# One sum of eight heads' softmax denominators in place of two sums of four, and a later place for the last one, in a fused attention and convolution kernel

## The chip, the cores and the metric

The kernel runs on one core of a Trainium2 chip, as one program. The metric is the device time of one execution, in microseconds (us). The compute engines are TensorE (PE, matrix products), VectorE (DVE), ScalarE (ACT) and GpSimd (Pool). SyncE (SP) computes nothing; its queue starts DMA transfers, as Pool's and ACT's queues can too.

## The reference

Two layers follow each other on an input of 4 images with 1024 channels and 32 x 32 pixels. The first is self-attention over the 1024 pixels (tokens) of an image, with 16 heads of 64 channels. The second is a bottleneck of three convolutions with batch normalization. All is float32. The change concerns the first layer, and in it the softmax:

```python
qkv = (x @ w_qkv.T + b_qkv).reshape(B, N, 3, nh, hd)
q, k, v = (qkv[:, :, 0], qkv[:, :, 1], qkv[:, :, 2])
q = _apply_rope(q, cos, sin)
k = _apply_rope(k, cos, sin)
q = _rmsnorm(q.reshape(B, N, inner), q_norm_w).reshape(B, N, nh, hd)
k = _rmsnorm(k.reshape(B, N, inner), k_norm_w).reshape(B, N, nh, hd)
scores = jnp.einsum('bqhd,bkhd->bhqk', q, k) * scale
attn = jax.nn.softmax(scores, axis=-1)
ctx = jnp.einsum('bhqk,bkhd->bqhd', attn, v).reshape(B, N, inner)
out = ctx @ w_proj.T
out = _rmsnorm(out, norm_out_w)
out = out + residual
```

After it come a 1x1 convolution to 256 channels, a 3x3 convolution and a 1x1 convolution back to 1024 channels, each with batch normalization over the whole batch, and a residual.

## The kernel before

The four images (batches 0 to 3) are worked through one after the other. For each of them the kernel projects q, k and v, does the attention, and projects the result with w_proj (the output projection, matmuls that the profile calls `p_y`). The four dense products of the layer use a Strassen-like scheme with seven products in place of eight, hence the many sums and differences on DVE.

Attention (`attention`) goes through two halves of 512 queries each (`c` = 0, 1), and in each half through eight pairs of heads (`hp` = 0 to 7). For a pair it makes eight score tiles `sc` of 128 keys by 2 heads by 512 queries (L781, four matmuls that share the array), ACT takes the exponential of each into `p` (L788), and DVE adds the eight tiles into one array of denominators of 128 partitions by 2 heads by 512 queries, `den` (L799 and L801). Then PE multiplies the eight tiles by v into `cx` (L810). The softmax is not divided before that product. Instead the context that comes out is multiplied by the inverse of its denominator later, in `mean_of_v`: a multiplication on DVE (L764) and the addition of v's bias on Pool (L765).

Before it can be inverted, a denominator has to be summed over the 128 partitions. This is a matmul with a matrix of ones, `dn`, into a bank of the pool `sc`, which has three tiles that go round. There are two ways:

- `sums_of_four`: four matmuls for the four heads of two pairs (L863), each with 128 partitions. `inverses` follows it: an ACT copy (L910), a transfer to DRAM and back into a shape with more partitions (L898, L902), a short reciprocal on DVE (L914), and transfers that spread each row over 64 partitions (L915, L932). The last group of a batch is treated by `last_inverses`, with a long reciprocal on DVE (L924) and Pool's queue for the transfers (L925, L932).
- `sum_of_eight`: `halve` first adds the upper 64 partitions of each pair's denominators to the lower 64 by accumulating DMAs on Pool's queue. For an even pair this is one copy (L873), for an odd pair two (L875 and then L876, which adds onto what L875 wrote). The result lies in a "home", one of the tiles T0 and T2. Four matmuls then do eight heads (L882), and the ACT copy is at L884 and the short reciprocal at L889.

Batch 0 uses the first way everywhere. Batches 1 to 3 use `sum_of_eight` in the first half of queries (`fold[0]`, two homes) and `sums_of_four` in the second half (`fold[1]` is None).

The order of the work is written out by hand: on PE, Pool, DVE and ACT the instructions stand in the order in which the program emits them. What is put off goes through lists. `late` holds sums of four, made after the second score tile of the next pair. `eights` holds sums of eight and `half_done` holds inversions, each with the number of the pair (8c + hp) at whose end it is due. `ready` holds spread inverses, taken by `mean_of_v` at the end of the next odd pair. In the projections, `after(n, step)` runs a step when n products have been done, where one matmul group of the output projection counts as half a product. `then` and `means` there are the differences for the first products and the `mean_of_v` of the last heads, on DVE. At each odd pair's end the program emits first `mean_of_v`, then `halve`, then what is due from the lists. `slow` puts the previous batch's residual additions (L1254, DMAs on Pool's queue) at pair ends.

The projections use the pools `o1` and `o2` of four banks each, in the same eight banks of PSUM as attention's `sc` and `cx`; a bank waits for its last reader.

Of the kernel before, what the change touches and what calls it, by code (L numbers as in the profile page):

```python
# [11 lines left out]
F32 = mybir.dt.float32  # L12
# [6 lines left out]
P = 128  # L19
# [66 lines left out]
def program(ctx, tc, x, wblk, w2, w3, vecs, cos, sin, out, bad):  # L86
# [71 lines left out]
    with tc.tile_pool(name=f"st{u}", bufs=2) as st, ExitStack() as s:  # L158
# [44 lines left out]
        def bank(kind, name):  # L203
            pool, shape = psum[kind]
            return pool.tile(shape, F32, tag=kind, name=name)
# [561 lines left out]
        def attention(b, c, q_all, k_all, v, probs_, late, ready, extra, slow, steps_in_all, load_parts, fold, then):  # L767


            at = half[c]  # L770
            sums_, contexts = [], []
            for hp in range(NHP):
                n = f"{b}_{c}_{hp}"
                rows = shifts(q_all, k_all, n, hp, c) if bad is None else None
                probs = []
                for t in range(N // P):
                    p = probs_[:, t]
                    sc = bank("sc", f"sc_{n}_{t}")
                    for keys in (low, high):
                        for j, d in enumerate((low, high)):  # L780
                            nc.tensor.matmul(  # L781
                                sc[keys, j], k_all[d, hp, t * P + keys.start : t * P + keys.stop], q_all[d, hp, at],
                                start=True, stop=bad is not None,
                            )
                    if bad is None:
                        for j in range(2):
                            nc.tensor.matmul(sc[:, j], ones[0:1, :], rows[j], start=False, stop=True)
                    nc.scalar.activation(p, sc, AF.Exp)  # L788
                    if t == 1:
                        if late:  # L790
                            late.pop(0)()
                        if fold and hp % 2 == 0:
                            d_ = fold[hp // 4][:, hp % 4 // 2 * 2 : hp % 4 // 2 * 2 + 2, :]
                        else:
                            d_ = acc.tile([P, 2, CH], F32, tag="tot", name=f"den_{n}")
                    if t == 3:
                        load_parts()
                    if t == 1:
                        nc.vector.tensor_tensor(d_, probs[0], p, ALU.add)  # L799
                    elif t > 1:  # L800
                        nc.vector.tensor_tensor(d_, d_, p, ALU.add)  # L801
                    probs.append(p)
                if (c, hp) == (NCH - 1, NHP - 1):
                    then()
                o = bank("cx", f"cx_{n}")
                for t in range(N // P):
                    for j in range(2):
                        h0 = (2 * hp + j) * HD
                        for i, keys in enumerate((low, high)):
                            nc.tensor.matmul(  # L810
                                o[j * HD : (j + 1) * HD, i], v[keys, t, h0 : h0 + HD], probs[t][keys, j],
                                start=(t == 0), stop=(t == N // P - 1),
                            )

                cx = q_all[:, hp, at]
                nc.scalar.copy(cx, o[:, 0])  # L816
                if b == 0 and (c, hp) != (NCH - 1, NHP - 1):
                    other = temp(f"cx_{n}")
                    nc.scalar.copy(other, o[:, 1])
                    nc.gpsimd.dma_start(cx, other, accum_op=ALU.add)  # L820
                else:
                    contexts.append((cx, o[:, 1]))
                sums_.append(d_)
                if hp % 2 == 1:
                    for r in ready:
                        mean_of_v(q_all, *r)
                    ready.clear()
                if fold:
                    halve(hp, d_, fold[hp // 4][:, hp % 4 // 2 * 2 : hp % 4 // 2 * 2 + 2, :])
                    if hp % 4 == 3:  # L830
                        eights.append((hp + 2, lambda n=n, hp=hp: sum_of_eight(b, n, hp, fold[hp // 4], ready)))
                if half_done and half_done[0][0] <= c * NHP + hp:
                    half_done.pop(0)[1]()
                if slow:
                    slow.pop(0)()

                if waiting:
                    next_waiting()
                slots = NCH * NHP - 1
                if extra and steps_in_all == 0 and hp > 0:  # L840
                    extra.pop(0)()
                for _ in range(len(extra) - -(-steps_in_all * max(slots - 1 - c * NHP - hp, 0) // slots) if steps_in_all else 0):
                    extra.pop(0)()
                if contexts:
                    nc.vector.tensor_tensor(contexts[0][0], *contexts.pop(0), ALU.add)
                if eights and eights[0][0] <= c * NHP + hp:
                    eights.pop(0)[1]()
                if hp % 2 == 0 or fold:
                    continue
                if (c, hp) == (NCH - 1, NHP - 1):  # L850
                    last_inverses(b, c, hp, n, sums_of_four(n, sums_), ready)
                else:
                    late.append(lambda n=n, hp=hp, ds=sums_: inverses(b, c, hp, n, sums_of_four(n, ds), ready))
                sums_ = []

        def sums_of_four(n, sums_):
            if n == f"0_{NCH - 1}_{NHP - 1}":
                bank("sc", f"skip_{n}")
            dn = bank("sc", f"dn_{n}")[:, 0]
            for i, d_ in enumerate(sums_):  # L860
                for j in range(2):
                    q = slice((2 * i + j) * QH, (2 * i + j + 1) * QH)
                    nc.tensor.matmul(dn[q, :], ones[:, :QH], d_[:, j], start=True, stop=True)  # L863
            return dn
# [10 lines left out]
                nc.gpsimd.dma_start(home[high], d_[high])  # L875
                nc.gpsimd.dma_start(home[high], d_[low], accum_op=ALU.add)  # L876

        def sum_of_eight(b, n, hp, home, ready):

            dn = bank("sc", f"dn_{n}")[:, 0]  # L880
            for i in range(4):
                nc.tensor.matmul(dn[i * QH : (i + 1) * QH, :], halves, home[:, i, :], start=True, stop=True)  # L882
            r = temp(f"rec_{n}")
            nc.scalar.copy(r, dn)  # L884
            k = 2 * b * NCH * NHP + 2 * (hp - 3)
            few, rows = to_few(n, k, 8, r[:: QH // 2, :])

            def invert():
                nc.vector.reciprocal(few, few)  # L889
                nc.sync.dma_start(rows, few)  # L890
                for i in range(2):
                    at = k + 4 * i
                    spread(0, hp - 2 + 2 * i, n + f"_{i}", ready, [dens[at : at + 2, :], dens[at + 2 : at + 4, :]])

            half_done.append((hp + 3, invert))

        def to_few(n, k, rows_, r):
            nc.sync.dma_start(dens[k : k + rows_, :], r)  # L898
# [6 lines left out]
        def inverses(b, c, hp, n, dn, ready):  # L905


            r = temp(f"rec_{n}")
            k = 2 * ((b * NCH + c) * NHP + hp - 1)
            nc.scalar.copy(r, dn)  # L910
            few, rows = to_few(n, k, 4, r[::QH, :])

            def invert():
                nc.vector.reciprocal(few, few)  # L914
                nc.sync.dma_start(rows, few)  # L915
                spread(c, hp, n, ready, [dens[k + j : k + j + 3 : 2, :] for j in range(2)])

            half_done.append((0, invert))

        def last_inverses(b, c, hp, n, dn, ready):  # L920
            k = 2 * ((b * NCH + c) * NHP + hp - 1)
            r = temp(f"rec_{n}")
            nc.scalar.copy(r, dn)
            nc.vector.reciprocal(r, r)  # L924
            nc.gpsimd.dma_start(dens[k : k + 4, :], r[::QH, :])  # L925
            spread(c, hp, n, ready, [dens[k + j : k + j + 3 : 2, :] for j in range(2)], nc.gpsimd)

        def spread(c, hp, n, ready, rows, queue=nc.sync):

            w = big_temp(f"inv_{n}")  # L930
            for j in range(2):
                queue.dma_start(  # L932
                    w[j * HD : (j + 1) * HD, :].rearrange("p (i t) -> p i t", i=2), rows[j].partition_broadcast(HD)
                )
            for i in range(2):
                ready.append((c, hp - 1 + i, w[:, half[i]]))
# [261 lines left out]
        for b in range(B):  # L1198
# [62 lines left out]
            fold = [None, None]  # L1261
            if b > 0:

                fold[0] = [tp.tile([P, NH, CH], F32, tag=t, name=f"den_{b}_{t}") for t in ("T0", "T2")]
            tc_, two = [], []

            def then(b=b, q_all=q_all, tc_=tc_, two=two):
# [428 lines left out]
```

## Time and profile before

| what | value |
|---|---|
| three runs | 2648.97, 2652.34, 2653.42 us; median 2652.34 |
| the profiled execution | 2650.94 us, of which its span 2649.1 us |
| PE busy | 2626.4 us (99% of the span) |
| DVE, ACT, Pool busy | 2143.2, 1120.7, 472.1 us |
| score tiles on PE (L781) | 456.4 us, products with v (L810) 338.2 + 112.7 us |
| `dn` on PE, four heads (L863) | 160 records, 23.2 us |
| bias of v on Pool (L765) | 56 records, 110.1 us, 1985 ns each |
| long reciprocal on DVE (L924) | 4 records, 3346 ns each |
| copies of `halve` (L873, L875, L876) | 12 each, 2.8 to 6.2 us from issue to landing |

The profile lists, for one execution, every instruction of every engine with its start, length, source line and tiles, the wait before it and what ended that wait. "Busy" is the time in which an engine worked on at least one instruction. A float32 matmul leaves two records, so a group of four `dn` matmuls has eight. Ends of matmuls are modelled. The granted clock of PE is given as a share of full speed; its mean over the execution was 0.998.

### The profile page before, as it was taken

How to read it: one execution, taken by the hardware profiler on the slowest of the kernel's cores; microseconds unless marked ns; L12 is line 12 of the kernel's file. 1: busy time of each engine (PE TensorE's matmuls, PEld its weight loads, DVE VectorE, ACT ScalarE, POOL GpSimd, SP SyncE). 2: the span in 40 equal slices, each digit the busy share in tenths (PEclk: the TensorE clock that was granted, in tenths of full speed). 3: DMA queues.
4: the chain of work that ended last, by engine and by line, in shares of the span. 5: the costliest groups of instructions: out<-in, count | busy, mean ns of one | idle time of the engine just before them, and what ended most of it. 6: DMA issues, size and time to landing. Idle time of an engine off the chain costs nothing. (4 is left out here: it accounts for less than half of the span.)

```text
span 2649.1 us, 40551 instructions
## 1 busy us (share of the span) xinstructions
PE 2626.4 (99%) x15446; PEld 1627.8 (61%) x15446; DVE 2143.2 (81%) x2595; ACT 1120.7 (42%) x1568; POOL 472.1 (18%) x592
## 2 busy tenths in 40 slices
PE   9999999999999999999999999999999999999997
PEld 4448533488888333688886333888884335846843
DVE  5567899998887877888879767987988779877987
ACT  2222566423442565333343565233525564312266
POOL 2542244301011221100111222000111221020000
PEclk9999999999999999999999999999999999999999
DMA  8887787777667451457775541765774443683175
GB/s 286 289 255 204 218 257 239 245 221 238 185 181 212 87 102 41 143 173 225 190 200 143 93 86 26 223 206 174 193 214 86 82 104 90 208 279 92 64 240 205
DMA packets 252939, 463.66 MB, mean 175 GB/s; under 512 B 32193, under 2 KB 125169, under 8 KB 252737
## 3 DMA queue, kind: packets, MB, share of 16 engines
q1 hardware_dynamic: 196816, 287.80, 34.7%
q0 software_dynamic: 47856, 156.40, 23.7%
q10 hardware_dynamic: 8064, 16.78, 1.8%
q8 instruction: 125, 2.05, 0.3%
q14 instruction: 78, 0.63, 0.1%
HBM read 329.53 MB, written 97.01 MB: 161 GB/s over the span
## 5 line engine op out<-in xcount | busy, mean ns | idle before, releaser
L788 ACT ACTIVATE p<-sc 128x1024 f32<-128x1024 f32 x512 | 478.2, 1047 | 17.7 <-PE sc L781 17.5
L781 PE MATMUL sc<-q,k 64*64 64x512 f32 x4096 | 456.4, 591 | 0.0
L801 DVE TENSOR_TENSOR den<-den,p 128x1024 f32<-128x1024 f32 x312 | 385.5, 1236 | 37.6 <-ACT p L788 5.1
L810 PE MATMUL cx<-p,to 64*64 64x512 f32 x3072 | 338.2, 589 | 0.0
L781 PEld LDWEIGHTS sc<-q,k 64*64 64x64 f32 x4096 | 149.3, 132 | 294.2 <-ACT p L788 150.6
L810 PEld LDWEIGHTS cx<-p,to 64*64 64x64 f32 x3072 | 117.5, 133 | 212.1 <-issue 210.8
L480 PE MATMUL p_v<-w_v,x 128*128 128x256 f32 x928 | 210.2, 379 | 1.4 <-DVE x L451 0.7
L485 PE MATMUL p_y<-q,w_y 128*128 128x256 f32 x928 | 209.8, 379 | 0.7 <-issue 0.7
L485 PEld LDWEIGHTS p_y<-q,w_y 128*128 128x128 f32 x928 | 176.0, 190 | 27.9 <-issue 4.1
L480 PEld LDWEIGHTS p_v<-w_v,x 128*128 128x128 f32 x928 | 176.1, 190 | 26.8 <-DVE x L451 1.7
L816 ACT COPY q<-cx 128x512 f32<-128x512 f32 x64 | 37.5, 586 | 348.0 <-PE cx L810 348.0
L765 POOL TENSOR_SCALAR q<-q,vec 128x512 f32<-128x512 f32 x56 | 110.1, 1985 | 290.2 <-DVE q L764 290.2
L485 PE MATMUL p_q<-to,w_q 128*128 128x256 f32 x672 | 152.2, 379 | 0.0
L485 PE MATMUL p_k<-to,w_k 128*128 128x256 f32 x672 | 152.2, 379 | 0.0
L485 PEld LDWEIGHTS p_q<-to,w_q 128*128 128x128 f32 x672 | 127.4, 190 | 18.4 <-issue 1.2
L485 PEld LDWEIGHTS p_k<-to,w_k 128*128 128x128 f32 x672 | 127.4, 190 | 18.4 <-issue 1.2
L810 PE MATMUL cx<-p,rq 64*64 64x512 f32 x1024 | 112.7, 589 | 0.0
L1600 PE MATMUL c<-h,w 128*128 128x512 f32 x256 | 110.3, 592 | 0.5 <-ACT h L1503 0.5
L799 DVE TENSOR_TENSOR den<-p 128x1024 f32<-128x1024 f32 x52 | 63.5, 1222 | 42.6 <-ACT p L788 42.6
L801 DVE TENSOR_TENSOR den_T<-den_T,p 128x1024 f32<-128x1024 f32 x72 | 88.2, 1225 | 7.5
L485 PE MATMUL p_y<-to,w_y 128*128 128x256 f32 x384 | 90.1, 379 | 0.6 <-PE p_y L485 0.6
L727 POOL DMA_DIRECT2D k<-ks x64 | 57.9, 1093 | 181.6 <-ACT p L788 70.9
(499 smaller groups left out, 4340.0 us busy)
## 6 DMA issues: line engine op xcount, KB each, us to landing
w_v<-wd2f SPq DMA_DIRECT2D x112, 256.0 KB, 3.2
w_y<-wd2f SPq DMA_DIRECT2D x112, 256.0 KB, 3.3
w_q<-wd2f SPq DMA_DIRECT2D x84, 256.0 KB, 3.0
w_k<-wd2f SPq DMA_DIRECT2D x84, 256.0 KB, 2.9
wd2f<-w_pre POOLq DMA_DIRECT2D x68, 256.0 KB, 4.5
q<-qs POOLq DMA_DIRECT2D x64, 256.0 KB, 5.5
k<-ks POOLq DMA_DIRECT2D x64, 256.0 KB, 4.7
x1df<-y POOLq DMA_DIRECT2D x32, 512.0 KB, 5.2
```

The costliest lines, as they stand in the source:

```text
L480: nc.tensor.matmul(o[:, q].rearrange("p (g f) -> p g f", g=2), r[:, i, q * P : (q + 1) * P], wt[:, :, i, :], skip_group_check=True, **at,)
L485: nc.tensor.matmul(o[:, q], wt[:, q, i, :], r[:, i, :], skip_group_check=True, **at)
L727: nc.gpsimd.dma_start(dst[i::2, f, :], other[1 - i :: 2, :], accum_op=ALU.add)
L765: engine.tensor_scalar(cx, cx, col("bv", hp), None, ALU.add)
L781: nc.tensor.matmul(sc[keys, j], k_all[d, hp, t * P + keys.start : t * P + keys.stop], q_all[d, hp, at], start=True, stop=bad is not None,)
L788: nc.scalar.activation(p, sc, AF.Exp)
L799: nc.vector.tensor_tensor(d_, probs[0], p, ALU.add)
L801: nc.vector.tensor_tensor(d_, d_, p, ALU.add)
L810: nc.tensor.matmul(o[j * HD : (j + 1) * HD, i], v[keys, t, h0 : h0 + HD], probs[t][keys, j], start=(t == 0), stop=(t == N // P - 1),)
L816: nc.scalar.copy(cx, o[:, 0])
L1600: nc.tensor.matmul(os[i], w3t[k][f // NH][:, f % NH, :], h2[b, k][:, half[c]], start=(k == 0), stop=(k == NPT - 1),)
```

## The change

In batches 1 and 2 the second half of queries gets one home too (`fold[1] = homes[:1]`, tile T0), for its first four pairs. Their eight heads take `sum_of_eight`. Pairs 4 to 7 have no home and stay with `sums_of_four`.

Sums of eight and inversions now carry due numbers that depend on the half, and two new places look at the lists inside a pair: after the third score tile for `half_done`, after the sixth for `eights`. With the numbers of the second half (+0.5 and +1.5) the sum of pairs 0 to 3 stands after the sixth score tile of pair 4, and its inversion after the third of pair 5. The inversions of sums of four carry the number of the next pair where they had 0.

The last group (pairs 6 and 7) of batches 1 and 2 is emitted by `after(0.5, ...)`, which is after the first matmul group of the output projection, and takes a bank of `o2`. In batches 0 and 3 it stays where it was. An unused bank that batch 0 allocated before its last sum is gone.

```diff
             sums_, contexts = [], []
+            homes = fold
             for hp in range(NHP):
+                fold = homes if homes and hp // 4 < len(homes) else None
...
                     nc.scalar.activation(p, sc, AF.Exp)
+                    if t == 2 and half_done and half_done[0][0] < c * NHP + hp:
+                        half_done.pop(0)[1]()
+                    if t == 5 and eights and eights[0][0] < c * NHP + hp:
+                        eights.pop(0)[1]()
...
-                sums_.append(d_)
+                if not fold:
+                    sums_.append(d_)
...
                     halve(hp, d_, fold[hp // 4][:, hp % 4 // 2 * 2 : hp % 4 // 2 * 2 + 2, :])
                     if hp % 4 == 3:
-                        eights.append((hp + 2, lambda n=n, hp=hp: sum_of_eight(b, n, hp, fold[hp // 4], ready)))
+                        home = fold[hp // 4]
+                        eights.append(
+                            (c * NHP + hp + (2, 0.5)[c], lambda n=n, hp=hp, home=home: sum_of_eight(b, c, n, hp, home, ready))
+                        )
...
                 if (c, hp) == (NCH - 1, NHP - 1):
-                    last_inverses(b, c, hp, n, sums_of_four(n, sums_), ready)
+
+                    def last(ds=sums_):
+                        last_inverses(b, c, hp, n, sums_of_four(n, ds), ready)
+
+                    if 0 < b < B - 1:
+                        after(0.5, last)
+                    else:
+                        last()
...
         def sums_of_four(n, sums_):
-            if n == f"0_{NCH - 1}_{NHP - 1}":
-                bank("sc", f"skip_{n}")
-            dn = bank("sc", f"dn_{n}")[:, 0]
+            dn = bank("o2", f"dn_{n}") if "o2" in psum else bank("sc", f"dn_{n}")[:, 0]
...
-        def sum_of_eight(b, n, hp, home, ready):
+        def sum_of_eight(b, c, n, hp, home, ready):
...
-            k = 2 * b * NCH * NHP + 2 * (hp - 3)
+            k = 2 * ((b * NCH + c) * NHP + hp - 3)
...
-                    spread(0, hp - 2 + 2 * i, n + f"_{i}", ready, [dens[at : at + 2, :], dens[at + 2 : at + 4, :]])
-
-            half_done.append((hp + 3, invert))
+                    spread(c, hp - 2 + 2 * i, n + f"_{i}", ready, [dens[at : at + 2, :], dens[at + 2 : at + 4, :]])
+
+            half_done.append((c * NHP + hp + (3, 1.5)[c], invert))
...
-            half_done.append((0, invert))
+            half_done.append((c * NHP + hp + 1, invert))
...
-                fold[0] = [tp.tile([P, NH, CH], F32, tag=t, name=f"den_{b}_{t}") for t in ("T0", "T2")]
+                fold[0] = homes = [tp.tile([P, NH, CH], F32, tag=t, name=f"den_{b}_{t}") for t in ("T0", "T2")]
+                fold[1] = homes[:1] if b + 1 < B else None
```

## The prediction

> **What bounds the kernel now.** I read the busy times of the page first.
>
> ```profile
> span 2649.1 us, 40551 instructions
> PE 2626.4 (99%) x15446; PEld 1627.8 (61%) x15446; DVE 2143.2 (81%) x2595; ACT 1120.7 (42%) x1568; POOL 472.1 (18%) x592
> ```
>
> TensorE (PE) is busy for 99% of the span and idle for 22.7 us. So the change can gain only the PE work it removes or the little idle time left, and any time for which it makes PE stand still comes straight off the end. The chain that ended last is made of PE rows in the attention stages too. So next I read the timeline of PE around the pairs of heads that the change touches: batch 1, second half of queries. Columns: start, length, engine, line, tiles.
>
> ```profile
> 1000.90 1.07 PE L863 MATMUL dn<-den,ones 128*32 128x512 f32 x8
> 1001.89 5.38 PE L781 MATMUL sc<-q,k 64*64 64x512 f32 x48
> ...
> 1013.96 7.05 PE L781 MATMUL sc<-q,k 64*64 64x512 f32 x64
> 1020.83 7.05 PE L810 MATMUL cx<-p,to 64*64 64x512 f32 x64
> 1027.69 1.90 PE L781 MATMUL sc<-q,k 64*64 64x512 f32 x16
> 1029.52 1.06 PE L863 MATMUL dn<-den,ones 128*32 128x512 f32 x8
> ```
>
> Eight score tiles start at 1013.96 (pair 3), their products with v at 1020.83, and pair 4 at 1027.69: 13.73 us for a pair, 6.87/8 = 0.86 for a score tile. Pair 2 ran from 999.02 to 1013.96 = 14.94; it holds one sum of denominators (L863, 1000.90). So a group of denominators costs PE 14.94 - 13.73 = 1.2 us.
>
> The changed sum also waits for copies made by GpSimd (Pool), so I read Pool's timeline where the same thing already happens: pair 7 of the first half, same batch, whose PE work starts at 956.71.
>
> ```profile
> 970.13 7.68 POOL L765 TENSOR_SCALAR q<-q,vec 128x512 f32<-128x512 f32 x4 [12.90 <-DVE q L764]
> 977.76 0.58 POOL L875 DMA_DIRECT2D den_T<-den  x1
> 981.08 0.84 POOL L876 DMA_DIRECT2D den_T<-den  x1 [2.74 <-DMA den_T<-den]
> 981.61 3.73 POOL L1254 DMA_DIRECT2D x1df<-in_x_dram  x4
> 1027.03 8.36 POOL L765 TENSOR_SCALAR q<-q,vec 128x512 f32<-128x512 f32 x4 [41.68 <-DVE q L764]
> ```
>
> The denominators were complete when VectorE (DVE) ended its last addition at 969.35. The first copy (L875) was nevertheless issued only at 977.76, when the four bias additions ahead of it in Pool's queue had ended (970.13 + 7.68 = 977.81). The second copy adds onto what the first wrote, so it waited until 981.08. How long the second takes to land is in the answer for its line:
>
> ```profile
> L876 POOL DMA_DIRECT2D den_T<-den x12: 802/808/843, 889.9 to 2117.4; - x12
> ...
> DMA to landing us min/median/max: 3.4/3.5/4.1
> ```
>
> In the present kernel nobody needs these copies for a pair and a half. The last view is the granted clock, in windows at the end of the kernel, where the last matmul ends at 2634.0 (columns: window, length, PE busy, clock, DMA share, GB/s):
>
> ```profile
> 2634.00:2635.00 1.00, 0.00 (x0) 1.00 0.99 406
> 2635.00:2636.00 1.00, 0.00 (x0) 1.00 0.22 86
> 2636.00:2637.00 1.00, 0.00 (x0) 0.51 0.00 0
> 2637.00:2638.00 1.00, 0.00 (x0) 0.50 0.00 0
> ```
>
> Two microseconds after PE fell idle its clock was halved.
>
> **What the Trainium skill says.** "TensorE: Matmul & The Clock Gate", Part 2, step 1: only weight loads are pulled ahead; matmuls stay in program order. So score tiles behind a waiting sum can't pass it. The same page, Part 1: GpSimd's queue is strict FIFO (the Pool rows above agree: 977.76 against 977.81), and after an idle window of about 3.4 us the array runs at half clock until about 4 us of sustained matmuls have passed. The trace agrees on the fall (1.00 to 0.50 within 2 us of idleness); it shows no recovery. "DMA: Bandwidth & Descriptors", Anatomy of one DMA: 2.0 us + bytes/436e3, an estimate of 2.6 us for these 256 KB; the trace has 2.9 (L875) and 3.5 (L876), which I use.
>
> **The change, part by part.** Pairs are counted 0 to 7 in the second half; times are those of batch 1 before, and in brackets batch 2.
>
> (a) The sums of pairs 0-1 and 2-3 (L863, inside pairs 2 and 4) become one sum of eight heads, after the sixth score tile of pair 4. One group less per batch: -1.2 (1581.66 - 1566.72 less 13.74 = 1.2), together -2.4. All later work moves up by 1.2.
>
> (b) The new sum's wait. PE comes to it at 1027.69 - 1.2 + 6 x 0.86 = 1031.6 [1595.40 - 1.2 + 5.15 = 1599.35]. Its third matmul needs the second copy of pair 3. In the new order Pool does four bias additions between pair 3's end and those copies. They start when DVE has done its first multiplication by the inverses of the first half's heads: 1027.03 - 1.2 = 1025.8 [1594.72 - 1.2 = 1593.5]. They take 8.36: 1034.2 [1601.9]. From first copy to second: 981.08 - 977.76 = 3.3 [3.2]: 1037.5 [1605.1]. Landing 3.5, and 0.1 to wake PE: 1041.1 [1608.7]. PE stands still for 9.5 [9.4] us, together +18.9. Behind it stand pair 4's last two score tiles and its products with v; for the tiles wait ScalarE's last two exponentials and DVE's last two additions. Nothing else can fill PE.
>
> (c) Clock. A gap of 9.5 us is nearly five times the 2 us after which the clock fell at the end. Four microseconds at half clock lose 2.0 us; together +4.0. Bounds: nothing if the clock holds or returns at once; 3.4 each if it takes two of the page's windows.
>
> (d) The last group (pairs 6-7) moves behind the first product of the output projection. Before, from the end of cx (1084.94) to the second product (1087.77) there are 2.83 us: group 1.11, product 1.72. After, the same two in the other order, but the second product now stands on the bank with cx's other half, which DVE reads until 1087.89 (L845). About +0.2 each, +0.4; bounds -0.4 and +1 each. The reciprocal (L924, 3.34) starts about 0.75 later, and so do the means of pairs 6-7; the waits for DVE there leave over 2 us, so PE pays nothing. That cover gone, up to 0.75.
>
> (e) Other waits. DVE's reciprocal of the eight sums now stands after pair 5's first addition, near 1055; its data is back about 5 us after the sum (ScalarE copy 0.6, two small SP transfers), near 1047: no wait. If it were late, all of pair 5's additions would stand behind it. The four multiplications at pair 5's end come about 7.5 us after that reciprocal, the spread rows after about 8.4 (from 1012.27 to 1013.84, four issues 2.41, landing 4.5): under 1 us of DVE idleness, in an engine with 2.4 us to spare in each pair. Nothing.
>
> (f) Queues. Pool gets six copies more per batch, 6 x 0.55 to 0.83 = 4 us of an engine that is 18% busy; residual loads (L1254) slip among them and are needed much later. SP issues three transfers less per batch. ScalarE has one copy less (0.59), DVE one short reciprocal less (0.24): both lie under PE. In batch 3 one reciprocal and two multiplications move up; Pool and PE keep their order: nothing. The dropped spare bank of batch 0 was never written; the sum keeps its bank, and the 0.7 us that the projection waits there stay.
>
> Sum: -2.4 + 18.9 + 4.0 + 0.4 = +20.9. Against the profiled execution, 2650.94 (span 2649.1 and 1.8 around it): 2671.8. The median of the three runs is 1.4 higher, so the forecast is 2652.3 + 20.9 = 2673 us.
>
> **Rivals.** First, the clock holds (0.13): as forecast without (c), +16.9, 2669. For it: no gap inside this kernel is that long, so no recovery is shown; against it the half clock of the tail.
> Second, a long recovery, or the delays in (d) and (e) reach PE as well (0.11): +3.4 per gap, or 1 to 2 us more per batch: 2676 to 2679. Against it: the slack counted in (d) and (e).
> Third, on the other side, the copies are not held up (0.05): if Pool issued them when the additions of pair 3 end (1026.25 - 1.2 = 1025.05) rather than after the bias additions, they'd land by 1025.1 + 3.3 + 3.5 = 1031.9, PE would wait 0.4 and its clock would hold: 2 x (0.4 - 1.2 + 0.2) = -1.2, 2651. It decides once the second copy lands before about 1032.6, where the wait equals the 1.0 saved. Against it: both batches' copies at pair 7 sat behind the bias additions, and the new order has them there again.
> Forecast: 0.69; 0.02 is left for what I don't see.
>
> **How the numbers follow.** The range takes the forecast with its landing times (3.4 to 4.1 us), the clock from nothing to 3.4 per gap, and (d): 2664 to 2680; outside lie the not-slower case and part of the long one. A measurement of this kernel can tell about 0.2%, 5.3 us, from no change. The not-slower case falls inside that: same 0.05, faster 0.01, slower 0.94.
>
> **What would show it.** In the changed profile, in batches 1 and 2: PE idle for about 9 us before the sum of eight heads in pair 4, released by a DMA into den_T; Pool's two copies right after four bias additions; matmuls in the following 4 us with a clock near 0.5; 192 instead of 208 instructions in the dn rows of PE; the last dn group after the first p_y product, PE waiting under 0.5 there. It is wrong if the copies are issued before the bias additions, if the sum finds them landed, or if PE gets back the lost time in a stage where it has no idle time to give.

## The result and the profile after

| | before | after |
|---|---|---|
| median of the runs | 2652.01 us (6 runs, 2648.91 to 2653.42) | 2671.68 us (6 runs, 2670.48 to 2674.53) |
| the profiled execution | 2650.94 us, span 2649.1 | 2671.87 us, span 2670.0 |

The ratio is 1.0077, with a 95% interval of 1.0066 to 1.0087. The change makes the kernel 19.7 us slower; the forecast was 2673 us, 20.9 us slower.

In the kernel after, line numbers below the attention loop's head have moved: the score tiles are L783, the products with v L816, the sums of four L878, the copies of an odd pair L890 and L891, the sum of eight L897. First the busy times of its page:

```profile
span 2670.0 us, 40523 instructions
PE 2632.7 (99%) x15430; PEld 1628.5 (61%) x15430; DVE 2144.6 (80%) x2593; ACT 1119.3 (42%) x1566; POOL 478.4 (18%) x604
```

PE was idle for 22.7 us before (2649.1 - 2626.4), and is idle for 37.3 now (2670.0 - 2632.7). That is 14.6 us of the 20.9 us of span; in the other 6.3 PE counts as busy, and yet it does 16 matmul records less. So PE does not only wait longer, it is slower somewhere too. Its waits say where it waits (columns: engine, tile and line, what it waited for, us in total, times, longest):

```profile
PE dn L897 <- DMA den_T<-den: 15.6, 2, 7.8
PE c2x L1477 <- DVE V L1412: 1.5, 2, 1.0
```

One new wait stands at the top, twice, once in each changed batch. The timeline of PE in batch 1 shows the place (start, length, engine, line, tiles, number of records, and in brackets the idle time before):

```profile
1022.04 7.05 PE L816 MATMUL cx<-p,to 64*64 64x512 f32 x64
1028.91 5.33 PE L783 MATMUL sc<-q,k 64*64 64x512 f32 x48
1034.17 1.05 PE L897 MATMUL dn<-den_T,halves 128*32 128x512 f32 x4
1043.05 1.92 PE L897 MATMUL dn<-den_T,halves 128*32 128x512 f32 x4 [7.83 <-DMA den_T<-den]
1044.90 3.41 PE L783 MATMUL sc<-q,k 64*64 64x512 f32 x16
1048.14 7.04 PE L816 MATMUL cx<-p,to 64*64 64x512 f32 x64
1055.01 7.04 PE L783 MATMUL sc<-q,k 64*64 64x512 f32 x64
...
1097.47 1.99 PE L485 MATMUL p_y<-q,w_y 128*128 128x256 f32 x8
1099.39 1.07 PE L878 MATMUL dn<-den,ones 128*32 128x512 f32 x8
1100.41 1.98 PE L485 MATMUL p_y<-q,w_y 128*128 128x256 f32 x8
```

Pair 4 starts at 1028.91. After six score tiles the first half of the sum runs (two of its four matmuls, in four records), then PE stands until 1043.05. From there the second half and the last two score tiles take longer than they should: 16 records of score tiles last 3.24 us (1044.90 to 1048.14), where eight tiles in 64 records take 6.87, so 1.72 for 16. Pair 5 starts at 1055.01: pair 4 took 26.10 us. Before, it started at 1027.69 and pair 5 at

```profile
1042.58 7.05 PE L781 MATMUL sc<-q,k 64*64 64x512 f32 x64
```

which makes 14.89 us. Further down in the kernel after, the last group stands behind the first product of the output projection, as the diff says.

What Pool did meanwhile is in its own timeline of the same stretch:

```profile
1028.16 8.11 POOL L765 TENSOR_SCALAR q<-q,vec 128x512 f32<-128x512 f32 x4 [12.23 <-DVE q L764]
1036.22 0.58 POOL L890 DMA_DIRECT2D den_T<-den  x1
1039.47 0.83 POOL L891 DMA_DIRECT2D den_T<-den  x1 [2.67 <-DMA den_T<-den]
```

It is the picture of pair 7 of the first half: four bias additions, then the first copy 0.05 us before the modelled end of the last of them, then 3.25 us until the second. The answer for L891 gives its landing:

```profile
who waited for it (us, times):
  PE dn L897: 15.6, 2
...
DMA to landing us min/median/max: 3.4/3.5/3.8
```

1039.47 + 3.5 = 1042.97, and PE goes on at 1043.05. Last, the granted clock of the stretch (columns: window, length, PE busy and records, clock, DMA share, GB/s):

```profile
1036.00:1038.00 2.00, 0.00 (x0) 0.92 0.32 68
1038.00:1040.00 2.00, 0.00 (x0) 0.50 0.31 64
...
1043.00:1044.00 1.00, 0.95 (x4) 0.50 0.00 0
...
1046.00:1047.00 1.00, 1.00 (x12) 0.50 0.05 16
1047.00:1048.00 1.00, 1.00 (x8) 0.55 0.09 16
1048.00:1050.00 2.00, 2.00 (x24) 1.00 0.07 12
```

The clock is halved during the gap and comes back at 1047.9 (a tenth of the window 1047 to 1048 was at full speed), 4.9 us after the matmuls resumed. In batch 2 the same gap is 7.79 us long, and pair 4 takes 25.40 us instead of 14.89. That is 0.70 us less than in batch 1: there the clock came back 3.5 us after the matmuls resumed.

### The profile page after: what moved, and what is told of

It reads as the page before. It is cut to its first block, busy times and chain, and to the rows that moved or that the text cites. A ratio compares the mean times of both kernels' runs of the same rounds, so it can differ in the third digit from the quotient of the medians.

```text
span 2670.0 us, 40523 instructions
## 1 busy us (share of the span) xinstructions
PE 2632.7 (99%) x15430; PEld 1628.5 (61%) x15430; DVE 2144.6 (80%) x2593; ACT 1119.3 (42%) x1566; POOL 478.4 (18%) x604
## 4 chain that ended last, share of the span: by engine, by line
PE 65%; DVE 2%; DMA 1%; ACT 1%; POOL 0%; issue 0%; DVEq 0%; POOLq 0%; ACTq 0%
PE cx L816 12%; PE sc L783 12%; PE p_y L485 10%; PE p_v L480 8%; PE p_k L485 6%; PE p_q L485 6%; PE c L1616 4%; PE c2x L1477 2%; PE c L1030 2%; PE c2y L1477 2%; PE c L989 1%; PE c1s L1030 1%; DMA den_T<-den 0%; DVE den L807 0%; DVE V L1412 0%; POOL q L765 0%
## 5 line engine op out<-in xcount | busy, mean ns | idle before, releaser
L790 ACT ACTIVATE p<-sc 128x1024 f32<-128x1024 f32 x512 | 478.1, 1049 | 19.1 <-PE sc L783 18.9
L783 PE MATMUL sc<-q,k 64*64 64x512 f32 x4096 | 458.5, 594 | 0.2 <-ACT p L790 0.2
L807 DVE TENSOR_TENSOR den<-den,p 128x1024 f32<-128x1024 f32 x288 | 355.7, 1235 | 49.4 <-ACT p L790 20.0
L816 PE MATMUL cx<-p,to 64*64 64x512 f32 x3072 | 338.2, 589 | 0.0
L783 PEld LDWEIGHTS sc<-q,k 64*64 64x64 f32 x4096 | 149.5, 132 | 297.5 <-ACT p L790 149.2
L816 PEld LDWEIGHTS cx<-p,to 64*64 64x64 f32 x3072 | 117.0, 133 | 213.1 <-issue 212.8
L807 DVE TENSOR_TENSOR den_T<-den_T,p 128x1024 f32<-128x1024 f32 x96 | 118.8, 1238 | 10.0
L816 PE MATMUL cx<-p,rq 64*64 64x512 f32 x1024 | 112.7, 589 | 0.0
L480 PE MATMUL p_v<-w_v,t 128*128 128x256 f32 x384 | 90.1, 379 | 0.0
```

What stands on the lines that cost most here:

```text
L480: nc.tensor.matmul(o[:, q].rearrange("p (g f) -> p g f", g=2), r[:, i, q * P : (q + 1) * P], wt[:, :, i, :], skip_group_check=True, **at,)
L783: nc.tensor.matmul(sc[keys, j], k_all[d, hp, t * P + keys.start : t * P + keys.stop], q_all[d, hp, at], start=True, stop=bad is not None,)
L816: nc.tensor.matmul(o[j * HD : (j + 1) * HD, i], v[keys, t, h0 : h0 + HD], probs[t][keys, j], start=(t == 0), stop=(t == N // P - 1),)
```

## The experiments

The theory is that of the prediction: in the new place the sum's last input lands late because both copies stand behind Pool's bias additions, and the gap halves the clock besides. The rivals are that the sum's place in pair 4 alone is at fault, that the moved last group takes part in the loss, or that the clock costs nothing. All edits are to the kernel after. Times are compared with the runs of the kernel before on the same chip; plus means slower, and the brackets hold the 95% interval of the ratio.

**The sum at the end of pair 4, after all its products with v**, 8.6 us of work later, with the copies where they were:

```diff
-    (c * NHP + hp + (2, 0.5)[c], lambda ...
+    (c * NHP + hp + (2, 1)[c], lambda ...
```

> The changed kernel, with the sum of eight heads in batches 1 and 2 made at the end of pair 4 (behind its products with v) rather than after the sixth score tile. Theory A, that the sum waits for copies which land about 9 us too late and that TensorE's clock then falls: the sum comes 8.6 us later, finds its copies landed to within about 0.5 us, the clock holds; 2650 us (2649 to 2652), PE idle before this sum under 1 us per batch. Theory B, that the loss lies in the moved last group or in the added copies' traffic: about 2670 us as before this edit.

Measured: 2650.93 us (12 runs) against 2652.10 (23 runs), ratio 0.9997 [0.9988, 1.0006]. The timeline of PE in this kernel, batch 1:

```profile
1034.57 7.05 PE L816 MATMUL cx<-p,to 64*64 64x512 f32 x64
1041.55 2.03 PE L897 MATMUL dn<-den_T,halves 128*32 128x512 f32 x8
1043.51 7.10 PE L783 MATMUL sc<-q,k 64*64 64x512 f32 x64
```

The sum is one block of eight records and lasts 2.03 us; about 1.0 of it is waiting, since 8 records without a wait take 0.99 (shown below in the fastest kernel). In batch 2 it lasts 1.30. The copies were no earlier than in the kernel after (the first at 1035.02 behind four bias additions, 7.31 us after the pair's start in both kernels; the second 11.24 us after it, 0.7 later than there), but now PE has other work until they land. The loss of 19.7 us is gone with one number changed.

**The copies ahead of the bias additions in Pool's queue**, with the sum where the change put it:

```diff
+    if fold and c == 1:
+        halve(hp, d_, fold[hp // 4][:, hp % 4 // 2 * 2 : hp % 4 // 2 * 2 + 2, :])
     if hp % 2 == 1:
         for r in ready:
             mean_of_v(q_all, *r)
         ...
-    if fold:
+    if fold and c == 0:
         halve(hp, d_, ...)
```

> The changed kernel, with one edit on GpSimd's queue: in the second half of queries the copies that fold a pair's denominators are issued ahead of the four bias additions of the same pair end. The sum of eight keeps its place after the sixth score tile of pair 4. Theory A: the copies start when pair 3's denominators are complete, the second lands 6.9 us later, within 0.5 us of when TensorE comes to the sum: PE idle there 0.2 to 1 us per batch, no fall of the clock, 2650 to 2652 us. Theory B (last group, or traffic of the copies, which are all still there): about 2670 us.

Measured: 2652.15 us (12 runs) against 2652.10, ratio 0.9999 [0.9991, 1.0008]. The timeline of Pool in this kernel:

```profile
1025.76 0.54 POOL L893 DMA_DIRECT2D den_T<-den  x1 [11.80 <-DVE den L807]
1028.96 0.81 POOL L894 DMA_DIRECT2D den_T<-den  x1 [2.66 <-DMA den_T<-den]
1029.55 6.72 POOL L765 TENSOR_SCALAR q<-q,vec 128x512 f32<-128x512 f32 x4
```

and of PE:

```profile
1026.91 5.33 PE L783 MATMUL sc<-q,k 64*64 64x512 f32 x48
1032.17 1.41 PE L900 MATMUL dn<-den_T,halves 128*32 128x512 f32 x8
```

The first copy now waits only for DVE's last addition of pair 3. It is issued 1.15 us before pair 4 starts instead of 7.31 us after, and the sum waits 0.4 us (in batch 2, where the block lasts 1.98, about 0.9). So either edit alone removes the loss: the place in Pool's queue makes the copies late, and the place of the sum makes PE pay for it. This kernel makes the third rival of the prediction real; that rival gave it 0.4 us of wait and 2651 us.

**The sum two score tiles earlier**, after the fourth:

```diff
-    if t == 5 and eights and ...
+    if t == 3 and eights and ...
```

> The changed kernel with the sum of eight heads after the fourth score tile of pair 4 rather than the sixth. TensorE comes to it 2 x 0.86 = 1.7 us earlier; when the copies land doesn't change. Theory A: it waits 1.7 us longer in each of two batches, 2671.7 + 3.4 = 2675.1 us. If the loss were a fixed cost of the sum at this place (bank, queue, last group): 2671.7 us.

Measured: 2675.89 us (4 runs) against 2651.55 (18 runs), ratio 1.0090 [1.0075, 1.0105], +24.3. Its waits:

```profile
PE dn L897 <- DMA den_T<-den: 19.0, 2, 9.5
```

That is 3.4 us more than the 15.6 of the kernel after, 1.7 for each batch, which is what two score tiles take. Pair 4 takes 27.54 and 27.95 us instead of 26.10 and 25.40, so 4.0 more in all: the 3.4 of wait, and 0.6 of half clock, which lasts longer in batch 2 here (its spells are listed in the last section). The losses of the two kernels differ by 4.7 us; the other 0.7 is well inside the interval, which is 4 us wide to either side. The sum's second half starts 14.14 us after pair 4's start (1033.09 to 1047.23), to the hundredth as in the kernel after (1028.91 to 1043.05). The landing sets the end of the gap in both places.

**The gap filled with useless matmuls**, to keep the clock up. Eight full matmuls go into the sum's bank ahead of the sum, which overwrites what they leave:

```diff
     dn = bank("sc", f"dn_{n}")[:, 0]
+    for _ in range(8 if c == 1 else 0):
+        nc.tensor.matmul(dn, ones, home[:, 0, :], start=True, stop=True)
     for i in range(4):
```

> The changed kernel, with eight matmuls of 128x512 of no use (about 6.9 us of TensorE, their result is overwritten) put ahead of the late sum in batches 1 and 2, so that TensorE is busy for most of its wait. If the clock's fall costs time on its own (theory A, 2.4 us in batch 1 and about 2.1 in batch 2): the remaining gap is about 1.5 us, the clock stays at 1.0 and the time is 2667 us. If the recorded fall costs nothing, or if the time is lost elsewhere: 2671 to 2672 us.

Measured: 2669.36 us (4 runs) against 2652.10, ratio 1.0066 [1.0049, 1.0082], +17.3. Repeated with more runs, beside half as many useless matmuls (`range(4 if c == 1 else 0)`):

> The filled kernel (eight matmuls ahead of the late sum) once more beside the half filled one, in more rounds. Its trace showed the clock at 1.0 throughout and pair 4 shorter by 2.3 us in batch 1 and 1.7 us in batch 2: 4.0 us below the half filled kernel if the clock is what matters (2667.7), no difference if it isn't.

> As the filled kernel, but with four matmuls of no use ahead of the late sum, about 3.4 us of its wait. The copies land when they did. Theory A: a gap of about 4.5 us stays, in which the clock falls to 0.5, so that only the start of the cold stretch moves; 2671 to 2672 us, as the changed kernel without any filling. If filling as such, and not the clock, had made the filled kernel quicker: about 2670.5, half of its gain.

Measured: with eight, 2667.18 us (6 runs) against 2651.55, ratio 1.0060 [1.0048, 1.0072], +15.6; with four, 2671.55 us (6 runs), ratio 1.0075 [1.0063, 1.0087], +20.0. PE's timeline with eight:

```profile
1028.08 5.33 PE L783 MATMUL sc<-q,k 64*64 64x512 f32 x48
1033.34 7.13 PE L897 MATMUL dn<-den_T,ones 128*128 128x512 f32 x16
1040.40 1.05 PE L899 MATMUL dn<-den_T,halves 128*32 128x512 f32 x4
1042.23 1.05 PE L899 MATMUL dn<-den_T,halves 128*32 128x512 f32 x4 [0.77 <-DMA den_T<-den]
1043.21 1.95 PE L783 MATMUL sc<-q,k 64*64 64x512 f32 x16
```

and with four:

```profile
1035.16 1.05 PE L899 MATMUL dn<-den_T,halves 128*32 128x512 f32 x4
1040.41 1.92 PE L899 MATMUL dn<-den_T,halves 128*32 128x512 f32 x4 [4.20 <-DMA den_T<-den]
1042.26 3.57 PE L783 MATMUL sc<-q,k 64*64 64x512 f32 x16
```

With eight, only 0.77 us of the gap is idle, the clock stays at 1.00, and the second half of the sum takes 0.98 us from start to start instead of 1.85, the two score tiles 1.77 instead of 3.24 (1044.98 is the next start). Pair 4 takes 23.76 and 23.71 us instead of 26.10 and 25.40: the clock cost 2.34 + 1.69 = 4.0 us. The medians agree: 19.7 - 15.6 = 4.1 (the first of the two comparisons gives 2.4, with four runs). In the repetition all six runs with eight (2665.89 to 2669.35) lie below all six with four (2669.57 to 2672.39). With four, PE stands 4.2 us instead of 7.8, the resumption is as late as ever (14.14 us after the pair's start), and the work after it is as slow as in the kernel after. Here a gap about half as long costs the whole of the half clock.

**Without the moved last group** (the move switched off, all else as in the kernel after):

```diff
-    if 0 < b < B - 1:
+    if False:
         after(0.5, last)
```

> The changed kernel without the move of the last group: pairs 6 and 7 of batches 1 and 2 are summed at the end of attention again. Theory A: only the 0.2 us per batch that the move costs are won back, 2671.3 us, with the same 8.9 us between the sum's halves. If the moved last group carries the loss: near 2650 us.

Measured: 2673.17 us (4 runs) against 2652.10, ratio 1.0080 [1.0063, 1.0097], +21.1. It missed: I had counted the move as a cost of 0.2 us a batch, and without it the kernel is, if anything, slower. Its waits show why:

```profile
PE dn L897 <- DMA den_T<-den: 15.6, 2, 7.8
PE p_y L485 <- issue: 2.2, 3, 0.8
```

The first product of the output projection waits 0.75 us in three batches; in the kernel before and the kernel after it does so once, in batch 0. The profile names no releaser here ("issue"), so the reason is read from the program. The tiles of the pool `sc` go round. With one group less in a batch the last sum lies in another tile, in banks that the first product of the projection takes over, so that the product has to wait for ACT's copy of the sum. The experiments with a spare bank, below, test this. The kernel after escapes this, because its last sum, made in the projection, lies in a bank of `o2`.

**The moved last group alone** (no eights in the second half):

```diff
-    fold[1] = homes[:1] if b + 1 < B else None
+    fold[1] = None
```

> The changed kernel without the sum of eight in the second half (no home there), only with the last group of batches 1 and 2 inside the output projection. Theory A: plus 0.2 us per batch against the kernel before, 2652 to 2652.5 us, no difference that can be measured. If the move had a gain or a loss of its own in PE's waits: a gap of over 1 us at the start of the output projections of batches 1 and 2.

Measured: 2652.78 us (13 runs) against 2652.63 (41 runs), ratio 0.9999 [0.9991, 1.0007]. The move has no cost that these runs can tell. As far as they tell, the eight heads with their early sum are the whole loss.

**Both cures together, and the last group back in its old place.** The sum at the end of pair 4, the copies first, no move; and, in batch 0, a 1x1 matmul into a bank of `sc` that nobody reads, so that the last sum goes one tile further:

```diff
     def sums_of_four(n, sums_):
+        if n == f"0_{NCH - 1}_{NHP - 1}":
+            s = bank("sc", f"skip_{n}")
+            nc.tensor.matmul(s[0:1, 0, 0:1], ones[:, 0:1], ones[:, 0:1], start=True, stop=True)
         dn = ...
```

> The parts that should gain, without those that lose: copies ahead of the bias additions, the sum of eight at the end of pair 4, the last group of batches 1 and 2 back at the end of attention, and in batch 0 one small matmul into the spare bank, so that the last sum gets the bank that the second product of the output projection uses and not that of the first. Theory A: two groups less (-2.3), no wait for the copies, and the 0.7 us before the first product of batch 0 gone: 2652.0 - 3.0 = 2649.0 us. If the short reciprocal in pair 5 now holds DVE up, or the added copies slow others: 2651 to 2653 us.

Measured: 2650.98 us (13 runs) against 2651.55, ratio 0.9997 [0.9988, 1.0005]. It missed too, and on the same point; its timeline of PE at the end of batch 1's attention:

```profile
1085.87 1.07 PE L884 MATMUL dn<-den,ones 128*32 128x512 f32 x8
1087.69 3.69 PE L485 MATMUL p_y<-q,w_y 128*128 128x256 f32 x16 [0.75 <-issue]
```

The product starts 0.1 us after ACT's copy of the sum has ended (1087.01 + 0.58 = 1087.59), as the reading of the banks says:

```profile
1087.01 0.58 ACT L944 COPY rec<-dn 128x512 f32<-128x512 f32 x1 [0.41 <-PE dn L884]
```

In batch 0 the wait is gone, in batches 1 and 2 it has come, 1.5 us in all. A spare bank in these two as well is one condition:

```diff
-        if n == f"0_{NCH - 1}_{NHP - 1}":
+        if n.endswith(f"_{NCH - 1}_{NHP - 1}") and n[0] in "012":
```

> The version with all gaining parts, mended: the small matmul into a spare bank stands ahead of the last sum in batches 1 and 2 as well as in batch 0, so that the first product of the output projection no longer waits for the copy out of the last sum's bank (0.75 us in each of batches 1 and 2 of the version before). If that wait is what ate part of the gain: 1.5 us below that version, 2649 to 2649.5 us, and no such wait in the profile. If not: 2651 us.

Measured: 2649.02 us (13 runs, 2646.85 to 2651.64) against 2652.63 (41 runs), ratio 0.9987 [0.9979, 0.9995]. The timeline of PE, batch 1:

```profile
1033.11 7.05 PE L816 MATMUL cx<-p,to 64*64 64x512 f32 x64
1040.09 1.06 PE L903 MATMUL dn<-den_T,halves 128*32 128x512 f32 x8
1041.08 7.10 PE L783 MATMUL sc<-q,k 64*64 64x512 f32 x64
...
1083.62 1.05 PE L884 MATMUL dn<-den,ones 128*32 128x512 f32 x6
1084.61 3.72 PE L485 MATMUL p_y<-q,w_y 128*128 128x256 f32 x16
```

The sum of eight finds its input there (0.99 us from start to start), and the projection starts without a wait. This kernel is 3.6 us faster than before. Counted: one group less in two batches, -2.3, and batch 0's wait of 0.7 removed make -3.0. It is a small gain, but the whole interval of the ratio lies below 1. The other way round the bank, both cures with the last group in the projection for batches 1 and 2 and the spare bank in batch 0 alone:

> The same parts, but with the last group of batches 1 and 2 inside the output projection, as the change has it, in place of the spare bank there. The first product doesn't wait for the copy, the second for DVE's use of its bank (0.2 us per batch): 2649.5 us, equal to the version with spare banks within what can be measured. If the move itself costs more than those 0.2: 2650.5 or above.

Measured: 2649.75 us (21 runs) against 2652.63, ratio 0.9990 [0.9984, 0.9997]. The two do not differ by more than their spread.

## Why the prediction was right

The terms, from the traces of before and after (batches 1 and 2 together):

| step | predicted | measured |
|---|---|---|
| (a) one group less | -2.4 | -2.3: pair 2 takes 13.79 instead of 14.94, each |
| (b) the new sum's wait | +18.9 | +17.7 |
| (c) half clock | +4.0 | +4.0 |
| (d) last group moved | +0.4 | +0.4 |
| (e), (f) other waits, queues | 0 | 0 |
| sum | +20.9 | +19.8; medians +19.7 |

(b) From the start of the sum's first half to that of its second 8.88 us pass in batch 1 and 8.84 in batch 2, with a sum that would take 0.99 in one piece and whose second half alone takes 0.98 at full clock. So each gap costs about 8.9 us, of which 7.8 is idle, where the prediction said about 9; the rest is that two halves apart take as long as two whole sums. The prediction counted all the time from PE's arrival to the landing as a wait, although by its own account the first two matmuls don't need the late copy and run in that time. That this is nearly the cost all the same was luck: the second half, alone behind the gap, takes as long as a whole sum, which the prediction didn't know. The term was mis-sized by 1.2 us: PE came to the sum 5.26 us after the pair's start where 5.15 was counted, and the copies landed 14.14 us after it where 14.6 was counted, mainly because the four bias additions took 8.11 us, not 8.36. The mechanism is shown by the runs: the end of the gap stays at 14.14 us after the pair's start when the sum is moved or the gap is partly filled; the gap goes when the copies are issued before the bias additions; and the loss goes when PE has other work until the landing. That matmuls behind a waiting one do not pass it ("TensorE: Matmul & The Clock Gate", Part 2, in the Trainium skill) agrees with this trace: the last two score tiles of the pair start only after the sum, at 1044.90.

(c) The size was right in sum, by halves of 2.34 and 1.69. The same page, Part 1, names an idle window of about 3.4 us and some 4 us of sustained matmuls; here the clock was back 4.9 and 3.5 us after resumption, near the page's time. The fall does not keep to 3.4 us: it came 2.45 and 4.49 us after the last matmul (by its modelled end), and 2.0 at the end of the kernel before, which the prediction took for agreement. With that the first rival (the clock holds, 2669) falls: the run with the gap filled shows what the kernel would be with the clock held, and it is 4 us faster. The second rival's long recovery did not come, nor did its delays in (d) and (e).

(d) From the first of the two groups to the second product it is 2.94 us after (1097.47 to 1100.41) and 2.72 before (1085.05 to 1087.77, by the lines below, with 1.72 for a product).

```profile
1085.05 1.07 PE L863 MATMUL dn<-den,ones 128*32 128x512 f32 x8
1086.05 3.72 PE L485 MATMUL p_y<-q,w_y 128*128 128x256 f32 x16
```

So the number was right, but the 0.2 us is not where the prediction put it. It expected the second product to wait for DVE's reading of its bank. That product starts 1.02 us after the group, as closely as a product did before (1.00). It is the group that comes late, 1.92 us after the first product and not 1.72; why is not shown by any run. DVE's reading (L855) ends at 1100.31, only 0.1 us before the product, so an earlier group might have met the expected wait instead. The long reciprocal waited 0.84 us for ACT's copy of the sum, the means 0.5, and PE in no place for them. The step also overlooked what the move saves: with one group less, leaving the last group where it was would have put its sum into the banks of the first product, 0.75 us a batch. The prediction looked at the bank only for batch 0, where nothing changes.

(e) The reciprocal of the eight sums stands at 1059.23 without a wait, and the four multiplications of pair 5 at 1067.22 without one. (f) The dn rows of PE hold 192 records:

```profile
L878 PE MATMUL dn<-den,ones 128*32 128x512 f32 x128 | 18.4, 605 | 0.9 <-DVE den L807 0.9
L897 PE MATMUL dn<-den_T,halves 128*32 128x512 f32 x64 | 12.3, 661 | 15.6 <-DMA den_T<-den 15.6
```

The two spans differ by 20.9 us and the terms sum to 19.8. The missing 1.1 lies outside the changed stretches. Where pair 2 of batch 1's second half starts, the trace of after is already 2.37 us late (1001.39 against 999.02), of which 1.95 come from the first product of the kernel (the second starts at 21.33 and before at 19.38). Between the two changed stretches another 0.25 is lost, and behind the second about 1.5 is won back. The medians, of six runs each, give 19.7. That the difference of the two spans equals the forecast is thus partly luck.

## What to carry to other kernels

Before moving a consumer earlier, follow its last producer through the queue it stands in: here two DMA issues of 0.58 and 0.83 us sat behind 8.1 us of additions that could wait, and either putting them first or placing the consumer at the end of the same pair takes the whole loss away. In this kernel, whose PE is 99% busy and in order, the unfilled gap was paid in full, and again through the clock. Removing one user of a rotating pool of banks shifts those behind it, so look at which bank the next stage takes first.

## What the runs showed of the hardware that was not expected

- In these traces the clock moves on a grid of 3.41 us. With half-microsecond windows, the spells at half clock in the kernel after last from 1037.67 to 1047.91 (10.24 us) and from 1617.93 to 1624.76 (6.83); with four useless matmuls from 1038.76 to 1045.58 (6.82) and from 1619.02 to 1622.43 (3.41); with the earlier sum from 1041.28 to 1051.52 (10.24) and from 1621.54 to 1631.78 (10.24). All are one, two or three times 3.41, and in each of the three kernels the two spells start 580.26 us apart, which is 170 times 3.4133, though the gaps start 578.2 to 579.4 us apart. The return came 3.5 to 5.2 us after matmuls resumed, the fall 2.4 to 4.5 us after they stopped (2.0 at the end of the kernel before). So the same gap costs 1.7 or 2.3 us depending on where it falls on that grid, and a gap of 4.2 us was enough for the fall. That gap is the one with four useless matmuls; in its batch 2 the clock fell 0.2 us after the matmuls had resumed (1618.82), and was low for 3.41 us all the same.
- A bank that is only allocated, as the spare bank of batch 0 in the kernel before, leaves the wait of 0.7 us in place; one 1x1 matmul into it removes the wait. Why is not shown by a run of its own.
- Four matmuls of 32 columns over one bank take 0.99 us together, and two of them alone take 0.98. A sum that is cut in two by a wait therefore costs a second 1.0 us. That the four share the array only when they run together would explain it; no run tests that.
